# Decoder layer on one core: first sequence's loads moved ahead of the front's end, late gates held back, filter tables ranked later

## The chip, the cores and the metric

The kernel runs on one core of one Trainium2 chip. Its time is the device time of one execution in microseconds (us). Before the change three runs gave 2112.03, 2112.74 and 2116.0 us; the median is 2112.74.

An engine works through its own instructions in order. The names used are PE (TensorE, the matrix engine), DVE (VectorE), ACT (ScalarE), POOL (GpSimd) and SP (SyncE, which here only issues transfers). Everything is in 32-bit floats.

## What is computed

The input x holds 16 sequences of 512 tokens with 256 channels. Each sequence goes through three blocks, each followed by a residual add and a layer norm:

```
z    = rmsnorm(u, pre_norm_w) @ in_proj_w.T          # 768 channels
z    = causal conv of length 3 along time + bias     # per channel
x2, x1, v = split(z, 3)
h    = sum_s residues[:, s] * exp(log_poles[:, s] * t)
y    = causal_conv(x1 * v, h) + x1 * v * D_skip      # 512 taps, per channel
y    = (y * x2) @ out_proj_w.T + u
x    = layernorm(x + y + mlp(rmsnorm(y, post_norm_w)))
x    = layernorm(x + self_attention(x) + cross_attention(x, ctx))
x    = layernorm(x + low_rank_mlp(x))
```

The long convolution (y) is the only step that is done for all sequences together: channel by channel, with the times of all 16 sequences as columns.

## The kernel before

**Two programs in a row.** The *front* (L368 to L966) computes x1 * v and the gates x2 for all sequences, then the long convolution, and leaves the results in DRAM: `yconv` (one tensor for each half of 128 channels, called half 0 and half 1 here) and `gates`. The *main part* (L970 on) takes the sequences one after another through the rest: it loads x, gate and y of a sequence (L1097 to L1100), multiplies y by the gate (`times_gate`, L1103), projects (`outp`, L1117), adds x (`add_op`, L1067), and goes on to the norm, the MLP (L1143 and L1195), attention and the last MLP.

**The planner.** Each program is written as a list of operations with engines, a cost, a priority (a low number goes first), the buffers read and written, and sometimes extra dependences (`after`). `Plan.schedule` (L103) places them with these costs: each engine takes its first startable operation by priority, a buffer class such as `"x"` has a fixed number of tiles, and a tile is given back when its last user is done. What comes out is a fixed order of instructions for each engine; on the chip every engine follows its list, and waits where something isn't ready. The costs and priorities thus set the order, and nothing else.

**The front's work.** For each sequence b, `prepare` (L440) loads x, norms and transposes it into xT, a tile of class `"x"` (ten tiles `fx` of 4 KB a partition). `project` (L473) makes 128 of the 768 channels: four matmul records on PE (L479), one pass on ACT (L486), two on DVE (L494). `x1v` (L502) makes two projections for one half of the channels, multiplies them on POOL (L506), transposes on PE (L512) and copies into `xv0` or `xv1`. `gate_of` (L523) makes the two gate projections and stores them (L535).

The first seven sequences are done whole, with priorities 100 b and below. The last nine (LATE) get half 0 first; half 1 and their gates follow at 3000 + 100 b. Of these nine, sequences 7 to 10 park xT in DRAM (`normed`, L551) and read it back (L562); 11 to 15 (KEPT) hold their tile. The gates of 14 and 15 (LAST) come at the very end, behind the last matmul of the convolution (L776).

The tables: `h` is built from 16 exponentials on ACT for each half (L613) and as many multiply-adds on DVE (L623, first step L621), at priority 160, and stored in DRAM as `hpad`. The convolution works in eight blocks of 32 channels, four for each half (loop at L648). A block loads four tables (`toe`, 512 KB each, L661, on SP) into tiles of class `"x"`, or into the space of xv0 in the last block; POOL zeroes their acausal triangle (L671, "cut" below); PE makes the states of earlier chunks (`near_mm`, L686), the triangular part (L737) and the part from the states (`far_mm`, L749, "far field"). ACT and DVE copy the result out of PSUM (L301, L299), and SP, in the last three blocks ACT too, stores it (L768).

**Queues.** SP issues nearly all transfers in the order of the plan, and waits at its head where one isn't ready. The main part's first loads stand behind the front's last stores.

## Time and profile before

| | |
|---|---|
| median of three runs | 2112.74 us |
| the profiled execution's own time | 2110.95 us |
| its span, first to last instruction | 2109.2 us |
| mean granted PE clock | 0.987 |
| PE busy | 2013.7 us, 95% of the span |
| DVE, ACT, POOL busy | 62%, 48%, 36% |
| last front matmul ends, first main matmul starts | 283.03 us, 292.07 us |
| second add of the first sequence (L1067) | 298.86 us |

Times in the timeline count from the span's start. A row of a timeline has start, duration, engine, line, operation, out<-in, shapes and count; the bracket at its end is the time for which the engine idled before it, and what it waited for. In the list of waits the numbers are us in total, times, longest. In the table by windows the columns after the window are its length, the busy time of PE, PE's weight loads, DVE, ACT and POOL with counts, the granted PE clock, the DMA engines' mean busy share, and GB/s.

The page's 40 slices are 52.7 us each. PE stands at 9 tenths from the eighth slice on; slices 5, 6 and 7 (211 to 369 us) hold 8, 7 and 8, and in slice 6 the granted clock's row has an 8. This is the end of the front and the start of the main part.

### The profile page before, as it was taken

How to read it: one execution, taken by the hardware profiler on the slowest of the kernel's cores; microseconds unless marked ns; L12 is line 12 of the kernel's file. 1: busy time of each engine (PE TensorE's matmuls, PEld its weight loads, DVE VectorE, ACT ScalarE, POOL GpSimd, SP SyncE). 2: the span in 40 equal slices, each digit the busy share in tenths (PEclk: the TensorE clock that was granted, in tenths of full speed). 3: DMA queues.
4: the chain of work that ended last, by engine and by line, in shares of the span. 5: the costliest groups of instructions: out<-in, count | busy, mean ns of one | idle time of the engine just before them, and what ended most of it. 6: DMA issues, size and time to landing. Idle time of an engine off the chain costs nothing.

```text
span 2109.2 us, 35600 instructions
## 1 busy us (share of the span) xinstructions
PE 2013.7 (95%) x14324; PEld 1034.7 (49%) x14324; DVE 1317.1 (62%) x1899; ACT 1020.7 (48%) x1414; POOL 758.2 (36%) x1020
## 2 busy tenths in 40 slices
PE   8899878999999999999999999999999999999977
PEld 4455545444554545454545454544545454545433
DVE  7976522736584848484847575766656675746463
ACT  7764521565426262717172626262535354466664
POOL 6785522243424241414141424242323232334342
PEclk9999989999999999999999999999999999999999
DMA  5366861030304040313131313222221313030300
GB/s 190 112 199 210 272 191 50 1 122 17 117 11 140 14 132 22 122 32 120 34 109 45 106 48 93 61 86 68 72 81 61 93 49 95 19 105 22 102 11 21
DMA packets 114935, 182.16 MB, mean 86 GB/s; under 512 B 13393, under 2 KB 62034, under 8 KB 114642
## 3 DMA queue, kind: packets, MB, share of 16 engines
q1 hardware_dynamic: 113234, 177.26, 27.0%
q10 hardware_dynamic: 1536, 2.62, 0.4%
q8 instruction: 113, 1.85, 0.4%
q14 instruction: 52, 0.43, 0.1%
HBM read 111.09 MB, written 68.76 MB: 85 GB/s over the span
## 4 chain that ended last, share of the span: by engine, by line
PE 81%; ACT 7%; POOL 4%; DVE 3%; issue 3%; DMA 2%; SPq 0%; ACTq 0%; POOLq 0%; DVEq 0%
PE mm L1143 14%; PE scores L1387 10%; PE mm L1296 9%; PE mm L1195 8%; PE scores L1491 7%; PE av L1526 7%; PE mm L1716 4%; PE mm L1224 3%; PE av L1732 3%; PE mm L1056 3%; PE fmm L479 2%; ACT ex L1503 2%; PE mm L1118 2%; PE mm L348 2%; PE mm L1578 2%
## 5 line engine op out<-in xcount | busy, mean ns | idle before, releaser
L1503 ACT ACTIVATE ex<-scores 128x2048 f32<-128x2048 f32 x160 | 300.2, 1876 | 165.4 <-PE scores L1491 161.3
L1143 PE MATMUL mm<-xT,w_l 128*128 128x512 f32 x640 | 298.1, 607 | 0.0
L1514 POOL TENSOR_SCALAR_AFFINE_SELECT ex<-ex 128x512 f32<-128x512 f32 x256 | 158.6, 638 | 355.2 <-ACT ex L1503 330.8
L1387 PE MATMUL scores<-keys,q 32*128 32x320 f32 (+4 forms) x2560 | 224.2, 455 | 11.8 <-ACT ex L1406 10.4
L1491 PE MATMUL scores<-q,keys 32*128 32x512 f32 (+3 forms) x2048 | 185.0, 464 | 17.3 <-ACT ex L1503 14.2
L1724 ACT ACTIVATE row<-mm,b_s 128x512 f32<-128x512 f32 x128 | 81.0, 685 | 233.0 <-PE mm L1716 232.9
L1143 PEld LDWEIGHTS mm<-xT,w_l 128*128 128x128 f32 x640 | 114.9, 190 | 143.7 <-issue 130.8
L1387 PEld LDWEIGHTS scores<-keys,q 32*128 32x128 f32 x2560 | 113.0, 184 | 147.2 <-issue 48.0
L1660 POOL TENSOR_TENSOR nd<-nd,nd 128x1024 f32<-128x1024 f32 x30 | 70.8, 2361 | 307.4 <-DMA nd<-di 307.4
L479 PE MATMUL fmm<-fx,inw 128*128 128x512 f32 x384 | 176.5, 602 | 4.1 <-DVE xv L299 1.5
L1526 PE MATMUL av<-ex,va 128*32 128x512 f32 (+3 forms) x2048 | 170.8, 442 | 0.0
L1432 DVE TENSOR_TENSOR scores<-scores,mask_qk 128x1024 f32<-128x1024 f32 x144 | 126.2, 876 | 63.8 <-PE scores L1387 60.6
L308 POOL TENSOR_SCALAR small<-small 128x4 f32<-128x4 f32 (+1 forms) x66 | 13.3, 201 | 423.0 <-DVE small L1026 393.7
L494 DVE SCALAR_TENSOR_TENSOR frow<-fmm,cw,frow 128x511 f32<-128x511 f32 x192 | 140.5, 744 | 37.7 <-ACT frow L486 33.5
L1195 PE MATMUL mm<-w_l,gT 128*128 128x256 f32 x640 | 160.8, 386 | 0.0
L1155 ACT ACTIVATE row<-mm 128x512 f32<-128x512 f32 x80 | 47.8, 598 | 223.9 <-PE mm L1143 223.9
L1491 PEld LDWEIGHTS scores<-q,keys 32*128 32x128 f32 x2048 | 90.0, 185 | 117.4 <-ACT ex L1503 42.2
L299 DVE COPY row<-av 128x512 f32<-128x512 f32 x68 | 47.1, 692 | 157.9 <-PE av L1526 136.2
L1195 PEld LDWEIGHTS mm<-w_l,gT 128*128 128x128 f32 x640 | 117.8, 190 | 47.3 <-issue 33.7
L1041 ACT ACTIVATE xt<-xt,small 128x256 f32<-128x256 f32 x192 | 103.1, 595 | 76.6 <-POOL small L1034 76.6
L1302 DVE TENSOR_SCALAR q<-mm,bqc_s 128x512 f32<-128x512 f32 x62 | 46.5, 751 | 140.6 <-PE mm L1296 140.6
L1296 PE MATMUL mm<-xT,wqc_s 128*128 128x512 f32 x256 | 129.3, 617 | 0.0
(194 smaller groups left out, 3475.4 us busy)
## 6 DMA issues: line engine op xcount, KB each, us to landing
dn<-row SPq DMA_DIRECT2D x120, 256.0 KB
keys<-dk SPq DMA_DIRECT2D x64, 256.0 KB
nd<-dn SPq DMA_DIRECT2D x30, 512.0 KB
nd<-di SPq DMA_DIRECT2D x30, 512.0 KB
fx<-hpad SPq DMA_DIRECT2D x28, 512.0 KB
xt<-in_x SPq DMA_DIRECT2D x16, 512.0 KB
gate<-gates SPq DMA_DIRECT2D x16, 512.0 KB
yt<-yconv SPq DMA_DIRECT2D x32, 256.0 KB
```

Of the source, the lines that this page charges most:

```text
L479: nc.tensor.matmul(ps.t, inw[:, k, bass.ts(m, P)], xT.t[:, k, :], start=(k == 0), stop=(k == KD - 1))
L494: lambda e, lag=lag: nc.vector.scalar_tensor_tensor(t.t[:, lag:], ps.t[:, 0 : T - lag], cw[:, m, 2 - lag : 3 - lag], t.t[:, lag:], ALU.mul ...
L1041: nc.scalar.activation(x.t[:, c, :], x.t[:, c, :], AF.Identity, bias=st[:, c, 9:10], scale=st[:, c, 8:9])
L1143: nc.tensor.matmul(ps.t, w[:, k, bass.ts(f, P)], zT.t[:, k, :], start=(k == 0), stop=(k == KD - 1))
L1195: nc.tensor.matmul(ps.t[:, bass.ts(cc, D)], gT.t[:, f, bass.ts(c, P)] if f < NF else gE.t, w_l3[:, f, :] if f < NF else w_l3e[:, c, :], st ...
L1296: nc.tensor.matmul(ps.t, w[:, k, cols], xT.t[:, k, :], start=(k == 0), stop=(k == KD - 1))
L1387: nc.tensor.matmul(sc.t[:, r, at : at + hi - lo], q.t[hd, bass.ts(i, P)], kk.t[hd, lo:hi], start=True, stop=True,)
L1432: nc.vector.tensor_tensor(diag, diag, mask, ALU.add)
L1491: nc.tensor.matmul(sc.t[:, r, at : at + T - j * P], keys[g].t[hd, TC + j * P : TC + (j + 1) * P], qas[g].t[hd, j * P :], start=True, stop= ...
L1503: lambda e, sc=sc, ex=ex: nc.scalar.activation(ex.t.rearrange("p (r n) -> p r n", r=HPG), sc.t, AF.Exp, scale=scale),
L1514: lambda e, ex=ex, at=at: nc.gpsimd.affine_select(out=ex.t.rearrange("p (r n) -> p r n", r=HPG)[:, :, at : at + P], in_=ex.t.rearrange("p ...
L1526: nc.tensor.matmul(av[g].t[bass.ts(r, SLOT), j * P :], va.t[:, j, h * VS : h * VS + SLOT], ex.t[:, r * T + at : r * T + at + n], start=(j ...
```

## The change

Four things are edited, all in the front and at its border.

1. Three lasting tiles, `early`, are opened ahead of the front. During the front they serve as the xT tiles of sequences 11, 12 and 13, and class `"x"` has seven tiles instead of ten. In the main part they are the one `gate` tile, the one `yt` tile and one of the five `xt` tiles, so the memory in use is the same.
2. At the end of the front's plan, x of sequence 0, its gate and half 0 of its y are loaded into them on SP (priority 5460), each after the last reader of the xT that the tile held; the main part's own loads for these three are empty. Half 1 of y is still a load of the main part.
3. The gates of sequences 10 to 13 get the priority 4700 + 100 b, 5700 to 6000, instead of 4000 to 4300. The blocks of half 1 have about 5400 to 5700.
4. The tables' exponentials, multiply-adds and stores get the priority 500 instead of 160.

```diff
+    early_ = ctx.enter_context(tc.tile_pool(name="early", bufs=1))
+    early = tiles(early_, "early", 3, [P, NT * D])
...
-            "x": tiles(fp_, "fx", 10, [P, R8 * P]),
+            "x": tiles(fp_, "fx", 7, [P, R8 * P]),
+            **{f"e{n}": [t] for n, t in enumerate(early)},
...
-        def as_xT():
-            return View("x", lambda t: t.rearrange("p (k n) -> p k n", k=KD))
+        def as_xT(b):
+            n = b - (B - KEPT)
+            return View(f"e{n}" if 0 <= n < 3 else "x", lambda t: t.rearrange("p (k n) -> p k n", k=KD))
...
-                gate_of(b, xT, 3000 + b * 100)
+                gate_of(b, xT, (3000 if b < B - LAST - 4 else 4700) + b * 100)
...
-                    160, r=[(LP, 0)], w=[ee],
+                    500, r=[(LP, 0)], w=[ee],
...
-                plan.op("DVE", 0.32, add, 160, r=[ee, (LP, 1), (LP, 2)], w=[h])
+                plan.op("DVE", 0.32, add, 500, r=[ee, (LP, 1), (LP, 2)], w=[h])
...
+        for n, (dst, src, deps) in enumerate((
+            (early[0].rearrange("p (c d) -> p c d", c=NT), x[0].rearrange("(c p) d -> p c d", p=P), ()),
+            (early[1], gates[0], (stores[0][1], stores[1][1])),
+            (early[2].rearrange("p (k j t) -> p k j t", k=KD, j=NT)[:, 0],
+             yconv[0][:, 0].rearrange("j p t -> p j t"), Y[0]),
+        )):
+            plan.op(
+                "SP", 0.6, lambda e, dst=dst, src=src: nc.sync.dma_start(out=dst, in_=src), 5460, w=[Buf(f"e{n}")],
+                lat=4.0, after=[*deps, *(o for _, o, _ in late_T[LATE - KEPT + n][1].seen)],
+            )
...
-        "yt": tiles(kept, "yt", 1, [P, KD, T]),
-        "gate": tiles(kept, "gate", 1, [P, KD * T]),
+        "yt": [early[2].rearrange("p (k n) -> p k n", k=KD)],
+        "gate": [early[1]],
...
-        "xt": tiles(kept, "xt", 5, [P, NT, D]),
+        "xt": [early[0].rearrange("p (c d) -> p c d", c=NT), *tiles(kept, "xt", 4, [P, NT, D])],
...
-        plan.op("SP", 0.5, load_x, p0 - 500, w=[x_], lat=4.0)
-        plan.op("SP", 0.5, load_g, p0 - 500, w=[gate], lat=4.0)
-        for k in range(KD):
+        plan.op("SP", 0.5, load_x if b else lambda e: None, p0 - 500, w=[x_], lat=4.0)
+        plan.op("SP", 0.5, load_g if b else lambda e: None, p0 - 500, w=[gate], lat=4.0)
+        if not b:
+            plan.op("SP", 0.5, lambda e: None, p0 - 500, w=[(yt, 0)], lat=4.0)
+        for k in range(0 if b else 1, KD):
             plan.op("SP", 0.5, lambda e, k=k: load_y(e, k), p0 - 500, w=[(yt, k)], lat=4.0)
```

`Y[0]` are the stores of half 0's `yconv`, `stores[0]` and `stores[1]` those of the gate of sequence 0.

More of the change, by code (lines that the diff above doesn't have):

```diff
@@ L468, in prepare @@
             scale_ops(x_, sq, pr - 120, "POOL" if b else "DVE")
-            xT = transposed(x_, lambda t: t, pr - 120, as_xT())
+            xT = transposed(x_, lambda t: t, pr - 120, as_xT(b))
             marks.append(plan.ops[-1])
@@ L558, in decoder_layer @@
             if b < B - KEPT:
-                xT = as_xT()
+                xT = as_xT(b)
                 plan.op(
@@ L627, in add @@
                         nc.vector.tensor_tensor(h.t[:, P - 1 : P], h.t[:, P - 1 : P], sk[:, k : k + 1], ALU.add)
-                plan.op("DVE", 0.32, add, 160, r=[ee, (LP, 1), (LP, 2)], w=[h])
+                plan.op("DVE", 0.32, add, 500, r=[ee, (LP, 1), (LP, 2)], w=[h])
             plan.op(
-                "SP", 0.4, lambda e, k=k, h=h: nc.sync.dma_start(out=hpad[bass.ts(k, P), :], in_=h.t), 160,
+                "SP", 0.4, lambda e, k=k, h=h: nc.sync.dma_start(out=hpad[bass.ts(k, P), :], in_=h.t), 500,
                 r=[h], w=[(HPAD, k)], lat=3.0,
@@ L634, in decoder_layer @@
         plan.op(
-            "SP", 0.4, lambda e: nc.sync.dma_start(out=hpad[D : D + 1, :], in_=zero_row), 160, w=[(HPAD, KD)],
+            "SP", 0.4, lambda e: nc.sync.dma_start(out=hpad[D : D + 1, :], in_=zero_row), 500, w=[(HPAD, KD)],
             lat=3.0,
@@ L646, in decoder_layer @@
         plan.op("ACT", 0.4, lambda e: nc.scalar.activation(aT, lpT, AF.Exp, scale=float(P)), 170, r=[(LP, "T0")], w=[(NEAR, "a")])
+        Y = [[] for _ in range(KD)]
         for blk in range(NR // R8):
@@ L755, in decoder_layer, with store @@
             for c in range(HPG):
-                o = View("row", lambda t: t.rearrange("p (q u) -> p q u", u=P))
+                res = View("row", lambda t: t.rearrange("p (q u) -> p q u", u=P))
                 plan.op(
                     "ACT DVE", (act(T), dve(T)),
-                    lambda e, c=c, o=o, ys=ys: copy(
+                    lambda e, c=c, o=res, ys=ys: copy(
                         e, o.t, ys[c].t.rearrange("p (q u) -> p q u", u=P)[:, :, ::-1]
                     ),
-                    pc + 5, r=[ys[c]], w=[o],
+                    pc + 5, r=[ys[c]], w=[res],
                 )
                 for par in range(2):
-                    def store(e, at=x0 + c * R8 + par * R8 // 2, par=par, kh=kh, o=o):
+                    def store(e, at=x0 + c * R8 + par * R8 // 2, par=par, kh=kh, o=res):
                         eng = nc.sync if e == "SP" else nc.scalar
@@ L771, in store @@
                         )
-                    plan.op("ACT" if par and blk >= NR // R8 - 3 else "SP", 0.6, store, pc + 10, r=[o], lat=3.0)
+                    o = plan.op("ACT" if par and blk >= NR // R8 - 3 else "SP", 0.6, store, pc + 10, r=[res], lat=3.0)
+                    Y[kh].append(o)
+        for n, (dst, src, deps) in enumerate((
[8 more added lines that the diff above has]
+            )
         for b, xT in last_gates:
```

## The prediction

> **What bounds the kernel now.** I read the page's first part, then the list of what PE waited for in the first 310 us, then the chain of waits and PE's timeline there.

> ```profile
> PE 2013.7 (95%) x14324; PEld 1034.7 (49%) x14324; DVE 1317.1 (62%) x1899; ACT 1020.7 (48%) x1414; POOL 758.2 (36%) x1020
> ```

> PE is busy for 95% of the span, so a gain must come out of the other 95 us or out of a low clock. By the built order the main part (from L1118 on) has the same PE instructions in the same sequence in both kernels; only tile names differ. All that can change lies before 300 us. PE's waits there:

> ```profile
> PE mm L1118 <- DVE yt L1105: 9.0, 1, 9.0
> PE fmm L348 <- DVE fx L333: 8.4, 2, 7.1
> PE fmm L512 <- POOL frow L506: 6.9, 7, 3.2
> ...
> PE fmm L686 <- issue: 2.5, 1, 2.5
> ```

> The largest is one wait of 9.0 us between the last front matmul and the first main one. The 8.4 us are the start, which stays. The third is mostly one place, which PE's timeline shows together with the first:

> ```profile
> 241.62 0.66 PE L512 MATMUL fmm<-ident,frow 128*128 128x128 f32 x4 [1.07 <-POOL frow L506]
> 245.44 1.12 PE L512 MATMUL fmm<-ident,frow 128*128 128x128 f32 x4 [3.16 <-POOL frow L506]
> 247.78 2.79 PE L686 MATMUL fmm<-xv,near 128*32 128x48 f32 x128 [1.22 <-DVE xv L299]
> ...
> 274.76 1.21 PE L749 MATMUL fmm<-xv,state 16*64 16x128 f32 x64
> 275.90 7.13 PE L479 MATMUL fmm<-fx,inw 128*128 128x512 f32 x16
> 292.07 6.75 PE L1118 MATMUL mm<-outw,yt 128*128 128x256 f32 x16 [9.04 <-DVE yt L1105]
> ```

> At the switch from channel half 0 to half 1 PE idles 1.07 + 3.16 + 1.22 = 5.45 us: no other projection is left to fill it. At the end, only four projections (7.1 us) stand between the last far-field group (its end, 275.97, is called t0) and the main part. The chain of waits says what was late:

> ```profile
> 236.12 6.80 DMA fx<-hpad
> ...
> 243.08 0.87 POOL fx L671
> ...
> 244.13 1.27 POOL frow L506
> 245.44 1.13 PE fmm L512 x4
> ...
> 283.62 7.53 DMA yt<-yconv
> ```

> First: a POOL product (L506) stands behind a POOL triangle cut (L671), which waits 6.80 us for a table. Second: the first sequence's loads are issued only at 282.6, and its y takes 7.53 us with 1.5 MB asked for at once.

> **The change, part by part.** Count from the second add of the first sequence (DVE L1067), 298.86 = t0 + 22.9; its followers keep their order.

> (a) End of the front. In the built order seven projections, not four, follow the last far-field group: one of sequence 12, two of 13, then 14 and 15. Warm ones cost 8.75/5 = 1.75 us, so PE is fed to t0 + 12.2; the three moved ones take 5.3 us out of the stretch before t0. SP now issues x in the middle of the last stores, the gate after the projection of 12 (t0 + 1.8), half 0 of y after those of 13 (t0 + 5.3), and only half 1 of y as a main load. What queues there: three last yconv stores stand behind the gate load on SP, and the half-0 load behind a gate store that needs DVE. Four ACT stores took 3.12 us (277.43) and held ACT's next projection by 2.7, so I put the ACT pass of 12's at t0 + 2.4, DVE's first pair at t0 + 3.2 to 4.7, the half-0 issue at t0 + 7, and the half-1 issue, behind two more gate stores, at t0 + 8.6. The landing of 256 KB alone is read from the key round trip, a store and then the load that waits for it:

> ```profile
> 353.34 0.65 SPq L1343 DMA_DIRECT2D dk<-row  x1
> 357.52 0.81 SPq L1349 DMA_DIRECT2D keys<-dk  x2
> 359.38 0.63 SPq L1343 DMA_DIRECT2D dk<-row  x1
> ...
> 364.48 0.80 SPq L1349 DMA_DIRECT2D keys<-dk  x2
> ```

> That is 4.2 and 5.1 us; the other end is the 7.53 above. The new loads share the queue with small stores, not with 2.5 MB of x, so I take 5.1: half 0 at t0 + 12.1, half 1 at t0 + 13.7. DVE's order is 9 of the 14 passes (0.74 each), product of half 0 (0.69), two passes, product of half 1, three passes, adds. So the half-0 product ends at 12.8, two passes at 14.3, the half-1 product at 15.0. Two of eight matmul steps need half 0 alone; the other six take 2.6 us warm (0.22 a matmul, as L1195's 20 in 4.48) or 5.1 at the cold rate of 292.07 (6.75/16); I take 3.9. Second add at t0 + 18.9 to 19, DVE being free at 17.2. Gain 22.9 - 19.0 = 3.9, plus the 5.3 = **9.2 us**. With 4.2 us and a warm clock the same working ends at t0 + 17.0, a gain of 11.2; with 7.5 and cold at 22.5, a gain of 5.7.

> The cold rate comes from rows:

> ```profile
> 245.00:250.00 5.00, 3.33 (x117) 2.96 (x120) 1.60 (x2) 0.00 (x0) 3.53 (x5) 0.50 0.96 391
> 265.00:270.00 5.00, 5.00 (x82) 4.88 (x75) 0.56 (x1) 0.00 (x0) 4.69 (x9) 0.74 0.85 225
> 292.00:296.00 4.00, 3.93 (x9) 3.17 (x10) 0.69 (x1) 0.00 (x0) 0.00 (x0) 0.50 1.09 359
> ```

> The third column from the end is the granted clock: 0.50 after the 9.04 us, but also after the 3.16 us gap, and 0.74 after 2.49 us of "issue". [...]

> (b) The switch. Sequence 10's two and 11's two gate projections (7.0 us) now stand around the last two transposes, and on POOL both last products come ahead of the cuts of half 1, so the 6.80 us DMA no longer stands before them. Before, the chain from the last projection (240.56) to L686 (247.78) took 7.2 us, of which 5.45 idle; with 7.0 us more work laid in it I leave 0.5 idle: 4.9. L686 at 2.79 for 128, where the warm run at 175.49 took 1.57, gives 1.2 more. **6.1 us**, between 2.3 (the 3.16 us wait and the low clock stay) and 6.7.

> (c) Tables behind five sequences. 32 exponentials (0.396 each) and 32 DVE steps (0.41) are only moved: 12.1 us of ACT, 13.5 us of DVE, from 20 to 66 us to about 30 to 110. PE's idle places in that stretch are 0.79 (36 us) and 5.43 (55 to 72 us). DVE is 36 of 40 us busy from 40 to 80, but 16.6 of 20 after, so half of it comes back as new waits: **3 us**, between 0 and 6. The first table is needed at 133, so its lateness costs nothing up to there.

> (d) Fewer tiles for the tables' blocks. fx has 7 tiles for 10; the three early ones hold sequences 11 to 13 until their gates are done. By the built order half 0's 16 loads turn through four tiles (fx0, 1, 5, 6) and half 1's 12 through five. PE's work in half 0 is then 16 x 0.98 + 4 x 1.2 + 3.4 + 17.5 + 2.6 = 44 us, 2.75 per load, 11 us a turn; less use 1.0, cut 1.1, issue 0.5 leaves 8.4 us for a landing, above the 6.80. In half 1 the shortest turn is about 8 us: 6.4 for the landing, just under 6.80. The trace doesn't show these rings. Now POOL's cuts wait 12.2 us in all for table landings, of which PE sees 0.7 (L737 on POOL); so the cost lies between 0 and 12.2. With tight turns at 6.80 I take a third: **-4 us**. A gain is excluded, since no tile is freed sooner.

> (e) The 2.49 us of "issue" at 260.8 comes in a run of over 150 short matmuls; the new order breaks some of these runs up. I take 0 (0 to 2.5 gained).

> Edits at nothing: loads of x and gate leave the main queue, the same bytes; lasting tiles take the place of the same three.

> Sum: 9.2 + 6.1 + 3 - 4 = 14.3 us. The profiled execution took 2110.95 (span 2109.2 and 1.75 around it), 1.8 below the median 2112.74. From the median: 2098.4, **2098**. Its own range is 2089 to 2107, two thirds of the way to either end of the terms: all best gives 11.2 + 6.7 + 6 + 2.5 = 26.4 (2086), all worst 5.7 + 2.3 - 12.2 = -4.2 (2117).

> **Rivals.**
> Give-back (0.17): the rings cost 8 us instead of 4, the tables bring nothing, the switch 4: 9.2 + 4 - 8 = 5.2, so 2107.5. For it: the DMA share is already 0.96 to 1.00 from 236 to 250. Against: eight gate projections, 2 MB of stores, leave half 0.
> The loads are late anyway (0.09), so that the change doesn't do what it says: half 1 of y stands on SP behind stores and gates, the idle 9 us comes back and eats (a): 14.3 - 9.2 = 5.1, so 2107.6. For it: four stores took 3.12 us at 277.43. Against: PE is fed 5.3 us longer than before.
> Starved rings (0.09), slower: table landings so slow that PE stands at L737. Place: the six turns (four in half 0, two in half 1). It takes the whole gain when the rings lose 14.3 + 4 = 18.3 us, and makes the kernel slower by over 0.2% from 22.5: 3.8 a turn, that is a landing of 8.4 + 3.8 = 12.2 us, where the longest in the chain is 6.80. Time from 2117; with a us more a turn 2123.

> **Chances.** Forecast 0.65. What a measurement of this kernel can tell from no change is about 0.2%, 4.2 us: faster means below 2108.5. That holds the forecast and about half of the two cases near 2107.5: 0.78; within 0.13; slower 0.09. The range reaches from 2088 to 2110, over those two cases, and leaves out the starved one and the ends.

> **What would show it.** Right: the wait of L1118's successor under 4 us; seven projections before it; L686 of half 1 at about 1.6 us for 128, no L512 wait over 2 us near it; the second add near 284.5. Wrong: L737 (or its heir) waiting on POOL for more than 2 us at a time: (d) too small; the first main DVE product waiting for its DMA past t0 + 16: (a); waits of L479 on DVE between 60 and 130 us: (c).

## The result, and the profile after

| | before | after |
|---|---|---|
| median of six runs side by side | 2112.39 us | 2101.86 us |
| lowest and highest | 2111.25, 2116.0 us | 2099.65, 2106.41 us |
| the profiled execution's own time, its span | 2110.95, 2109.2 us | 2099.65, 2097.9 us |
| second add of the first sequence | 298.86 us | 286.66 us |
| from the second add to the end of the span | 1810.3 us | 1811.2 us |

The changed kernel is faster: the ratio of the times is 0.9951 with a 95% interval of [0.994, 0.9961], so 10.5 us by the medians. The profiled execution of after is the fastest of its six; a second profile of the same kernel (below) is the slowest of its five. In after the heirs of the lines named in the prediction are L485 (projection), L518 (transpose behind L512's product), L694 (near), L745 (triangle), L757 (far field), L1129 (product with the gate), L1142 (first main matmul) and L1088 (add).

PE's busy time changed little, from 2013.7 to 2010.4 us, as it should where only waits go.

What PE waited for in the first 310 us of after (us in total, times, longest):

```profile
PE mm L1142 <- DVE early L1129: 5.7, 1, 5.7
...
PE fmm L745 <- issue: 4.3, 3, 2.0
PE fmm L518 <- POOL frow L512: 3.3, 3, 1.8
...
PE fmm L745 <- POOL fx L679: 1.3, 1, 1.3
```

The 9.0 us wait ahead of the main part is 5.7, and the 6.9 us behind POOL's products are 3.3. The line "issue", in which PE waits for nothing that the profile names, has grown. PE's timeline at the two places of the prediction:

```profile
231.89 1.88 PE L485 MATMUL fmm<-early,inw 128*128 128x512 f32 x4
233.70 1.57 PE L694 MATMUL fmm<-xv,near 128*32 128x48 f32 x128
...
262.93 5.42 PE L485 MATMUL fmm<-early,inw 128*128 128x512 f32 x12
268.18 7.03 PE L485 MATMUL fmm<-fx,inw 128*128 128x512 f32 x16
280.90 5.72 PE L1142 MATMUL mm<-outw,early 128*128 128x256 f32 x16 [5.69 <-DVE early L1129]
```

The near group of half 1 follows a projection with no bracket, so with no idle time, and takes 1.57 us for 128 where it took 2.79. Behind the last far-field group (t0 is now 263.00) there are seven projections instead of four. But main's first matmul still waits 5.69 us. The chain of waits says what for, and SyncE's timeline why it was late:

```profile
268.38 7.03 DMA early<-gates
...
275.48 4.54 DMA early<-yconv
```

```profile
267.59 0.65 SPq L776 DMA_DIRECT2D yconv<-frow  x1
268.38 1.00 SPq L792 DMA_DIRECT2D early<-gates  x1
...
272.90 0.72 SPq L541 DMA_DIRECT2D gates<-frow  x1
275.48 0.38 SPq L792 DMA_DIRECT2D early<-yconv  x1
...
277.44 0.37 SPq L1107 DMA_DIRECT2D early<-yconv  x1
```

The gate's load (512 KB) is issued 5.4 us behind t0, right behind stores that SyncE was still issuing until 268.24, and lands 7.03 us later. Half 0 of y is issued just then, 12.5 us behind t0. Two things stood before it: stores, the last of which was issued by 273.62 (t0 + 10.6), and then the gate's load itself, for which SyncE waited at half 0's issue (us in total, times, longest):

```profile
SPq L792 <- DMA early<-gates: 1.8, 1, 1.8
```

Half 0 does not read the gate. But in this trace SyncE's 634 transfers step eight semaphores, the gate's load and half 0's step the same one (number 106), and the 1.8 us are a wait for that one. Half 1 comes 2 us later, behind the last two gate stores.

Cut at the milestones, the two profiled executions give this ledger. A projection more or fewer done before a milestone is counted at 1.72 us.

| stretch | before | after | projections moved out | gain |
|---|---|---|---|---|
| start to the first near group of half 0 | 175.49 | 170.52 | 1 | 3.25 |
| on to the near group of half 1 | 72.29 | 63.18 | 3 | 3.95 |
| on to t0 | 28.19 | 29.30 | -1 | 0.6 |
| t0 to the second add | 22.89 | 23.66 | -3 | 4.4 |

The sum is 12.2 us, and 0.9 us of it is lost in the main part. By the prediction's own signs: seven projections stand before the main part, the near group of half 1 takes 1.57 us, and no wait for a product is over 2 us at the switch; but the wait ahead of the main part is not under 4 us, and the second add stands at 286.66 instead of 284.5.

### The profile page after: what moved, and what is told of

Same layout as the page of the kernel before. It is cut to its first block, busy times and chain, and to the rows that moved or that the text cites. A ratio compares the mean times of both kernels' runs of the same rounds, so it can differ in the third digit from the quotient of the medians.

```text
span 2097.9 us, 35560 instructions
## 1 busy us (share of the span) xinstructions
PE 2010.4 (96%) x14324; PEld 1031.2 (49%) x14324; DVE 1324.8 (63%) x1906; ACT 1015.8 (48%) x1407; POOL 756.1 (36%) x1020
## 3 DMA queue, kind: packets, MB, share of 16 engines
q8 instruction: 113, 1.85, 0.4%
## 4 chain that ended last, share of the span: by engine, by line
PE 86%; ACT 6%; POOL 2%; DVE 2%; issue 2%; DMA 2%; SPq 0%; ACTq 0%; POOLq 0%; DVEq 0%
PE mm L1167 14%; PE scores L1411 10%; PE mm L1320 9%; PE mm L1219 8%; PE scores L1515 8%; PE av L1550 7%; PE fmm L485 6%; PE mm L1740 4%; PE mm L1248 3%; PE av L1756 3%; PE mm L1077 3%; ACT ex L1527 2%; PE mm L1142 2%; PE mm L348 2%; PE mm L1602 2%
## 5 line engine op out<-in xcount | busy, mean ns | idle before, releaser
L1515 PE MATMUL scores<-q,keys 32*128 32x512 f32 (+3 forms) x2048 | 185.6, 466 | 17.2 <-ACT ex L1527 14.2
L308 POOL TENSOR_SCALAR small<-small 128x4 f32<-128x4 f32 (+1 forms) x66 | 13.1, 199 | 419.3 <-DVE small L1047 390.4
L299 DVE COPY row<-av 128x512 f32<-128x512 f32 x68 | 47.0, 691 | 158.2 <-PE av L1550 140.2
L485 PE MATMUL fmm<-fx,inw 128*128 128x512 f32 x312 | 142.7, 601 | 0.0
L1430 ACT COPY ex<-scores 128x2048 f32<-128x2048 f32 x48 | 89.5, 1865 | 55.3 <-PE scores L1411 48.3
```

The costliest lines, as they stand in the source:

```text
L485: nc.tensor.matmul(ps.t, inw[:, k, bass.ts(m, P)], xT.t[:, k, :], start=(k == 0), stop=(k == KD - 1))
L1430: "ACT", act(HPG * T), lambda e, sc=sc, both=both: nc.scalar.copy(both.t, sc.t), ps_ - 6,
L1515: nc.tensor.matmul(sc.t[:, r, at : at + T - j * P], keys[g].t[hd, TC + j * P : TC + (j + 1) * P], qas[g].t[hd, j * P :], start=True, stop= ...
```

## The experiments

All times are medians; ratios are to the kernel before, run on the same chip. That kernel's medians were 2112.37, 2112.59 and 2112.76 us in the three groups of runs. The first four kernels do one part alone or leave one out.

**One part alone: the tables.** The kernel before with edit 4 only.

```diff
-                    160, r=[(LP, 0)], w=[ee],
+                    500, r=[(LP, 0)], w=[ee],
```

(The multiply-adds and stores likewise.)

> The kernel before with one part of the change: the tables' exponentials, multiply-adds and stores at priority 500 instead of 160. My theory: the parts add up, and the tables are worth what the two traces show up to the first L686 of half 0 (175.49 against 170.52 us, less one projection of 1.7 us): 3.2 us, so 2109 against 2112.4 before, with L686 of half 1 still slow (about 2.8 us for 128) and the 9 us wait at the end unchanged. Rival: the tables earn nothing alone, since PE's waits at 55 to 72 us come back at 80 to 130: 2112. Second rival: the new order of the whole front that any changed priority brings is what pays: 2105 or less.

2111.91 us, ratio 0.9995 [0.9987, 1.0004]. The first near group starts at 172.37 against 175.49, with one projection (1.72 us) fewer done, so 1.4 us are gained there; but the wait ahead of the main part grew from 9.0 to 10.1 us and the second add stands at 298.23. Alone, edit 4 earns nothing that can be measured; the time is that of the first rival, and the theory's 2109 is out.

**One part alone: the held gates.** The kernel before with edit 3 only.

```diff
-                gate_of(b, xT, 3000 + b * 100)
+                gate_of(b, xT, (3000 if b < B - LAST - 4 else 4700) + b * 100)
```

> The kernel before with one part of the change: the gates of sequences 10 to 13 at priority 4700 + 100 b; ten fx tiles and all main loads as before. My theory: the idle 5.5 us at the switch of the halves and most of the low clock behind it go (about 4.5), and the three projections that now stand behind t0 cover part of the wait for the loads, which are issued later too: 3 more; together 2105. Rival: held gates only move the idle time to the end, where the loads start as much later as the projections last: 2108 or more, with a wait at L1118 of 9 us as before.

2108.7 us, ratio 0.9978 [0.9968, 0.9989]. PE's timeline of this kernel:

```profile
233.91 1.57 PE L686 MATMUL fmm<-xv,near 128*32 128x48 f32 x128
...
266.30 12.28 PE L479 MATMUL fmm<-fx,inw 128*128 128x512 f32 x28
287.43 5.40 PE L1118 MATMUL mm<-outw,yt 128*128 128x256 f32 x16 [8.85 <-DVE yt L1105]
```

The idle time at the switch of halves is gone, and the near group is at 1.57: held gates alone do that. At the end seven projections (12.28 us) now follow t0, and the wait is still 8.85: main's loads were issued at 275.91, later against t0 than before, since they stand behind the stores of the held gates. So at the end held gates alone only move the idle place along, as the rival said; in all they earn 3.7 us.

**All but the tables.** The changed kernel with edit 4 undone.

```diff
-                    500, r=[(LP, 0)], w=[ee],
+                    160, r=[(LP, 0)], w=[ee],
```

> The changed kernel with the tables back at priority 160; the rest as changed. My theory, parts that add up: 3.2 us slower than the changed kernel, 2105. Rival, tables worth nothing: 2102. If the tables were the whole gain of the front it would be 2109.

2107.43 us, ratio 0.9978 [0.997, 0.9987]: 5.6 us above the changed kernel, against 0.5 that the same edit earned alone. The first near group starts 4.7 us later (175.18), one projection more being done, so 2.9 us are lost there against that profile (1.7 against a second profile of the changed kernel, below). In half 1, 2.9 us of "issue" appear, at a place where such a wait lasted 0 to 3.17 us in other versions with the tables late (below). The stretch from t0 to the second add is about as long as in the changed kernel (23.8 us). None of the three times expected was met, 2107.43 lying between two of them. So the parts do not add up, and a part's worth depends on which others are there.

**All but the early loads.** The changed kernel without edit 2; the lasting tiles stay, and x, gate and both halves of y are main's own loads.

```diff
-        for n, (dst, src, deps) in enumerate((
...
-                "SP", 0.6, lambda e, dst=dst, src=src: nc.sync.dma_start(out=dst, in_=src), 5460, w=[Buf(f"e{n}")],
...
-        for k in range(0 if b else 1, KD):
+        for k in range(KD):
```

> The changed kernel without the three early loads: the lasting tiles, seven fx tiles, held gates and tables stay, PE's order is the same, and x, gate and both halves of y of the first sequence are loaded by the main part. My theory: the end gains from the early loads even though the gate's load landed late; four loads at 276 to 278 us land after about 8 us, so the first L1129 product stands near 285 instead of 280 and the kernel takes 2106 to 2107. Rival: the end's gain comes from the three held projections alone, and the early gate load is what makes half 0 late: 2102 or below, the same as the changed kernel.

2106.17 us, ratio 0.9972 [0.9962, 0.9983], above the changed kernel by 4.3, as the theory expected, but not for its reason: from t0 (267.97) to the second add it took 23.4 us, no more than the 23.66 of the changed kernel. The first product with the gate starts at 282.81, t0 + 14.8, where the changed kernel has t0 + 17.1. Its queue shows why: with the lasting tiles main's own load of x moved up to 243.52, the gate to t0 + 7.3, and half 0 of y to t0 + 8.7, ahead of where the early loads put it.

**The gate's load earlier.** The changed kernel with the tiles dealt out anew; x is loaded by main, behind half 1 of y.

```diff
-            (early[0].rearrange("p (c d) -> p c d", c=NT), x[0].rearrange("(c p) d -> p c d", p=P), ()),
-            (early[1], gates[0], (stores[0][1], stores[1][1])),
-            (early[2].rearrange("p (k j t) -> p k j t", k=KD, j=NT)[:, 0],
+            (early[0], gates[0], (stores[0][1], stores[1][1])),
+            (early[1].rearrange("p (k j t) -> p k j t", k=KD, j=NT)[:, 0],
```

> The changed kernel with the three lasting tiles dealt out anew: the gate of the first sequence goes into the tile of sequence 11, which is free at the switch to main, half 0 of y into the tile of sequence 12, and x is loaded by main behind half 1 of y. TensorE's order is that of the changed kernel. Theory (the 7.03 us of the late gate load, for which half 0 of y waited, made the first term short): half 0 of y is issued 5.5 to 7 us after the last far-field group instead of 12.5, the first product for main comes some 4 us earlier, the second add stands 20 to 21.5 us after that group instead of 23.66, and the time is 2 to 3 us under the changed kernel's, near 2099. Rival (half 1 of y, behind the last stores of gates, sets the end by itself): second add at 23 to 24 us, time within 1 us of the changed kernel's, or above it where x stands behind half 1.

2099.72 us, ratio 0.9942 [0.9929, 0.9955]. SyncE's timeline, with t0 at 267.90:

```profile
258.42 0.58 SPq L791 DMA_DIRECT2D early<-gates  x1
...
273.08 0.63 SPq L791 DMA_DIRECT2D early<-yconv  x1
...
280.39 0.37 SPq L1106 DMA_DIRECT2D early<-yconv  x1
```

Half 0 is issued at t0 + 5.2, a little earlier than expected, its product starts at t0 + 9.8, and the second add stands at t0 + 21.8 (20 to 21.5 expected), 1.9 us sooner than in the first profile of the changed kernel and 3.4 sooner than in the second. Half 1 is now what comes last (t0 + 12.5). The test changes two things at once: the gate's load is no longer ahead of half 0, and half 0, in the tile of sequence 12, stands further up the queue, ahead of three stores of y and two of gates. By the times it is 1.3 us under the changed kernel's pooled median (below), which is within the spread.

**Another load ahead of half 0.** The changed kernel with the gates of sequence 12 ahead of those of 11, so that x's load and not the gate's is the late one.

```diff
-                gate_of(b, xT, (3000 if b < B - LAST - 4 else 4700) + b * 100)
+                gate_of(b, xT, (3000 if b < B - LAST - 4 else 4300 if b == 12 else 4700) + b * 100)
```

> The changed kernel with one priority changed: the gates of sequence 12 come at the switch of halves and those of sequence 11 late, so that the gate load goes early and the load of x, also 512 KB, becomes the late one. If half 0 of y is held by whichever 512 KB load stands ahead of it on the queue, it is issued again 11 to 13 us after the last far-field group, and the time stays within 1 us of the changed kernel's. If it is the gate's own data that the first product waits for, the first product comes 2 to 4 us earlier and the time is 2 us lower, near 2100.

2104.87 us, ratio 0.9968 [0.9957, 0.9979], slower than the changed kernel by 3 to 4; neither expectation held whole. Half 0 was issued 6.06 us behind x's load (272.25, then 278.31); but x's load itself went out sooner, at t0 + 2.4, the stores ahead of half 0 were through at 277.51, only 0.8 us before half 0 went out, and the first product ended its wait 13.1 us behind t0 (269.82) instead of 17.1. The gain was lost at once: on DVE the last passes of the gates stood behind that product, and PE waited for one of them:

```profile
PE mm L1142 <- DVE frow L500: 4.3, 1, 4.3
```

From t0 to the second add it takes 24.0 us, so the 3 to 4 us were lost before t0. The stretch from the near group of half 1 to t0 takes 36.2 us here, and 29.3 in the first profile of the changed kernel; waits named issue make 6.6 us of it here and 3.1 there. What these waits are comes below.

**Late stores on another queue.** The changed kernel with ScalarE's queue taking second-half stores from one block earlier.

```diff
-                    o = plan.op("ACT" if par and blk >= NR // R8 - 3 else "SP", 0.6, store, pc + 10, r=[res], lat=3.0)
+                    o = plan.op("ACT" if par and blk >= NR // R8 - 4 else "SP", 0.6, store, pc + 10, r=[res], lat=3.0)
```

> The changed kernel with ScalarE's queue also taking the second-half stores of the fourth block from the end, which in the changed kernel stood on SyncE's queue behind loads of tables that waited for TensorE (7.6 us in two waits). If those late stores hold back the last copies and so the loads that follow, the copies that waited 3.09 and 1.73 us for stores wait under 1 us, the second add comes 1 to 3 us earlier and the time is 1 to 3 us lower, 2099 to 2101. Rival (the last copies are early enough): within 1 us, 2101 to 2103.

2100.56 us, ratio 0.9948 [0.9934, 0.9962]: the gate's load was issued at t0 + 4.2, half 0 at t0 + 8.9, and the second add stood at t0 + 22.3 (t0 is 262.78). As expected, the last copies of DVE no longer wait for stores. The stretch is 1.4 us shorter than in the first profile of the changed kernel; the times can't tell the two apart.

**The changed kernel again.**

> The changed kernel itself once more, for the spread of its profiled executions: 2102 by the median. If the unexplained idle time of TensorE (named issue in the waits, 0.80, 0.57 and 1.55 us in the second half of the near-field before) belongs to the order of the program, it comes back at the same places with the same lengths; if it varies from one execution to the next, it is found at other places or with other lengths, up to the 3.17 us of the version without the early loads.

2101.01 us, ratio 0.9942 [0.9928, 0.9957]. With the first six, eleven runs have a median of 2101.01 us. In this profile t0 is 267.12 and the second add stands 25.2 us behind it. The order of PE is the same as in the first profile, where t0 is 263.00. The idle times named issue sit at the same matmuls with other lengths. First profile, then second:

```profile
239.37 2.23 PE L745 MATMUL fmm<-fx,xv 128*64 128x128 f32 x37 [1.55 <-issue]
...
259.59 0.37 PE L757 MATMUL fmm<-xv,state 16*64 16x128 f32 x2 [0.57 <-issue]
```

```profile
241.19 3.86 PE L745 MATMUL fmm<-fx,xv 128*64 128x128 f32 x37 [2.17 <-issue]
...
263.71 0.38 PE L757 MATMUL fmm<-xv,state 16*64 16x128 f32 x2 [1.12 <-issue]
```

In both executions the first stands behind 42 block products, and the second before the last 2 of a far-field group of 64. The stall before the 47th of a near group was 1.21 and 0.66 us; that before the 49th was not there in the first profile and 0.45 us in the second.

**The program shifted.** What are these stalls? The changed kernel with 32 transposes more at the head of PE's program, and nothing else moved.

```diff
+                for _ in range(8):
+                    ps = Buf("mm")
...
+                        for c in range(NT):
+                            nc.tensor.transpose(ps.t[:, bass.ts(c, P)], ident, ident)
...
+                    plan.op("PE", 0.0, turn, -2000, w=[ps])
```

> The changed kernel with 32 more transposes (of the identity, into accumulators that nobody reads) at the head of TensorE's program; all that follows is in the same order. In all runs of this order so far the idle time named issue sits at the same matmuls, with lengths from 0.3 to 3.2 us: before the 47th of the 64 matmuls of one near group, the 43rd of the block products behind the near group of half 1, the 49th of a near group of 64, and the 63rd of a far-field group of 64. Counted along TensorE's program these stand 528, 378 and 126 matmuls apart. Theory (TensorE waits for its own instructions, which come in blocks of a fixed size of some 126 to 128 matmuls with their weight loads): each of these stalls moves 32 matmuls ahead, to the 15th, the 11th, the 17th and the 31st. Rival (each stall is a wait for data that the profile doesn't name, or belongs to the place in the program): the stalls stay at the 47th, 43rd, 49th and 63rd. Time: 2101 by either, up to 3.9 us more if the 32 transposes at 0.12 us lie bare.

2104.04 us, ratio 0.9956 [0.994, 0.9971]. Behind the near group of half 1, PE now stops after 11 block products instead of 42:

```profile
233.54 0.87 PE L754 MATMUL fmm<-fx,xv 128*64 128x128 f32 x11
238.04 5.63 PE L754 MATMUL fmm<-fx,xv 128*64 128x128 f32 x69 [3.63 <-issue]
```

That stall moved 31 matmuls ahead. The other three are gone, and so is one that the expectation leaves out (1.97 and 1.99 us, behind 28 block products of half 0); 32 matmuls ahead of their places nothing is seen. Three others appeared: 0.21 us before the second matmul of a group of block products, 0.20 us before the 63rd of the last far-field group, and 0.51 us before 16 block products at 262.49. So one of the four moves that the theory named came. Its distances also hold an error: from the 47th to the 43rd it is 504 matmuls, four times 126, not 528.

A count over all traces decides. Take PE's own instructions in their order: matmuls, weight loads and waits on semaphores. The 13 profiles of this case have 65 idle times of PE over 0.12 us named issue. Of these 54 come with 1473 or 1474, 1985, 2242, 3265 or 3266, 3522, 3777 or 3778, 4034, 4289 or 4546 instructions before it, whatever the version. Each of these counts leaves 193 or 194 when divided by 256. So the stalls belong to a count of 256 instructions, about 126 matmuls with their weight loads, and not to data. The queues' part of the after page says what is fetched (packets, MB, share):

```profile
q8 instruction: 113, 1.85, 0.4%
```

1.85 MB in 113 packets are 16.4 KB each. The traces hold the time of each packet of this queue:

| profile | PE stops | packet starts, ends | PE goes on |
|---|---|---|---|
| after | 237.81 | 236.95, 237.95 | 239.37 |
| the changed kernel again | 239.02 | 238.81, 239.72 | 241.19 |
| the program shifted | 234.41 | 235.77, 236.68 | 238.04 |
| without the early loads, again (below) | 254.30 | 255.31, 256.28 | 257.48 |

All 54 stalls end 0.9 to 1.6 us behind the end of such a packet. So, by these times and counts, what PE waits for is its own program, and a stall is long where the packet comes late; in these runs of short matmuls it lasted up to 3.63 us. The other 11 do not belong here: 0.80 to 0.86 us before the block products behind a near group, in ten profiles, which stays at its place in the shifted kernel too, and the 0.51 us above. What they wait for is open.

**Without the early loads, again.**

> The version of the changed kernel without the early loads, once more. Its median was 2106.17, against 2101.0 for eleven runs of the changed kernel, though counted from the last far-field group its second add came no later (23.4 us against 23.66 and 25.16). If the early loads earn those 5 us: 2105 to 2107 again, with the last far-field group some 3 us later than in the changed kernel. If the difference was the spread of executions: 2100 to 2103.

2103.9 us, ratio 0.9958 [0.9946, 0.9971]. t0 is 267.33, and the second add stands 23.4 us behind it, as in the first run of this version. The time lies between the two expectations. By the medians the early loads earn some 3 to 5 us, and none of it behind t0. The profiles show it ahead of t0: from the near group of half 1 to t0 this version takes 33.7 and 33.0 us, and the changed kernel, the tiles dealt out anew, the late stores and both together (below) take 28.5 to 32.2. Both profiles of this version have one stall in common:

```profile
257.48 0.38 PE L694 MATMUL fmm<-xv,near 128*32 128x48 f32 x16 [3.17 <-issue]
```

It is 3.17 us in both, and 0, 0.45, 0.29, 1.78, 1.40 and 0.85 us in the six unshifted profiles of versions with tables ranked late and early loads. Main's load of x goes out at 243.52 in the first profile of this version, between the tables' loads, where the early load waits until 255.81. That x's 512 KB crowd out the instructions there is argued, not shown: with the tables early (and x at 261.21) the stall was 2.90 as well, and the packet itself took 0.95 us, no longer than at short stalls; it started late. The stall also costs behind its end: the next 48 block products take 4.51 us in both profiles, at a granted clock of 0.65 and 0.57, and 2.84 us at 1.00 behind the stall of 0.85.

**Both shorter ends together.** The tiles dealt out anew and the stores on ScalarE's queue.

> The changed kernel with both edits that shortened the stretch behind the last far-field group: gate in the first tile, half 0 of y in the second and x loaded by main (21.76 us from that group to the second add, where the changed kernel had 23.66 and 25.16), and the second-half stores of the fourth block from the end on ScalarE's queue (22.29 us). If they add up: 20 to 21 us, and a time near 2098. Rival (both shorten the same wait, the late half 1 of y): 21.5 to 22.5 us and 2099.5 to 2101.

2099.45 us, ratio 0.9931 [0.9919, 0.9944], the fastest version measured. From t0 (264.08) to the second add it takes 20.3 us, so the two edits add up in this stretch, as expected; the time is 1.5 us above the 2098 expected, at the rival's lower end. DVE's timeline there:

```profile
279.67 0.68 DVE L1131 TENSOR_TENSOR early<-early,early 128x512 f32<-128x512 f32 x1
280.27 3.62 DVE L500 SCALAR_TENSOR_TENSOR frow<-fmm,cw,frow 128x510 f32<-128x510 f32 x5
283.81 1.28 DVE L1087 TENSOR_TENSOR y<-mm,early 128x512 f32<-128x512 f32 x2
```

No row has a bracket: DVE no longer waits for y, but works through the last gates' passes without a gap up to the adds, and PE waits 2.3 us for one of them. DVE is what sets the end now. The version's interval overlaps that of the changed kernel's rerun (0.9928 to 0.9957), so it isn't shown to beat that kernel.

## Why the prediction was right, and where it was wrong

The direction was right, and the time lies within the range. The forecast of 14.3 us was 3.8 above the 10.5 measured (2.9 above the 11.4 of the eleven runs). The forecast's own range is not what its words say: two thirds of the way from 2098.4 to the ends 2086 and 2117 is 2090 to 2111, not 2089 to 2107. Term by term:

**(a), the end of the front: 9.2 forecast, 4.4 and 2.9 measured.** This is the term that was mis-sized. The 5.3 us of moved projections came, but the 3.9 us of the shorter stretch did not. Set against seven projections, the stretch of the kernel before would be 22.89 + 5.16 = 28.1 us. Held gates alone give 26.5, the lasting tiles (with late tables) on top 23.4 and 23.4, and the early loads on top of these 23.7 and 25.2: no gain. The step that failed is "the gate after the projection of 12 (t0 + 1.8)" with "the half-0 issue at t0 + 7". The gate's load was issued at t0 + 5.4, behind late stores of y: the last copies of DVE waited 3.09, 1.36 and 1.73 us for earlier stores to free their buffers, and in the built order the last stores wait for these copies. The stores ahead of half 0 ended at t0 + 10.6, 3.6 us later than the forecast had it, and the wait for the gate's load held it for another 1.9 us, to t0 + 12.5 (10.7 and 12.0 in the second profile). The prediction had counted the stores behind the gate's load but not the lateness of those ahead of it, and it had not looked at the landing that an issue itself waits for. Its sign for this failure was given: the first main product waiting for its DMA past t0 + 16. It ran at t0 + 17.1. Where half 0 was issued at t0 + 5.2 (the tiles dealt out anew), the stretch fell to 21.8, and with the stores moved too to 20.3, which is near the 19.0 that (a) had worked out.

The landing itself was sized well: 5.1 us assumed for 256 KB, 4.54 measured. So were the last six matmul steps: 3.9 us assumed, 3.88 from the end of the half-1 product to the second add; in the second profile it was 5.6, over the 5.1 that the prediction gave for a cold clock.

For the matmuls behind the wait the prediction took a middle between the warm and the cold rate. In the version with the gate in the first tile, PE had only two gaps of 1.51 and 1.41 us ahead of the last 12 of main's first matmuls. The table by windows (columns as ahead of the prediction), first for that version before, around and behind the two gaps, then for the 16 behind the 5.69 us gap of after:

```profile
274.00:279.00 5.00, 5.00 (x13) 2.22 (x12) 3.84 (x7) 3.19 (x5) 0.00 (x0) 1.00 1.00 315
279.00:284.00 5.00, 2.21 (x7) 0.87 (x5) 4.11 (x8) 0.78 (x1) 0.00 (x0) 0.94 0.67 220
284.00:289.60 5.60, 5.47 (x12) 3.87 (x12) 4.24 (x7) 1.29 (x3) 0.00 (x0) 0.50 0.99 308
```

```profile
281.00:287.00 6.00, 5.62 (x16) 3.92 (x16) 4.88 (x8) 1.52 (x4) 0.00 (x0) 0.69 0.91 267
```

The granted clock, third from the end, is 1.00 before and 0.50 behind the two short gaps. Here gaps of 1.4 to 1.5 us in a thinly filled stretch (PE busy for 2.21 of 5.00 us) did not leave the matmuls behind them warm.

**(b), the switch of halves: 6.1 forecast.** The idle time went from 5.45 us to 0 and the near group from 2.79 to 1.57, which is 6.7, the upper end of the bounds. The held gates alone show the same lines.

**(c), the tables: 3 forecast.** The pair of profiles gives 3.25 up to the first near group, so the size looked right. Over all profiles it is less: with early tables that group starts at 175.18 to 176.70 us (three profiles), with late ones at 170.52 to 172.65 (nine, without the shifted program), 3.9 us apart in the mean, or 2.2 without the projection of 1.72. And alone the edit earned 0.5 us, and taken out of the changed kernel it cost 5.6. The step that failed is the sum itself, which gave the tables one price whatever else is changed.

**(d), fewer tiles: -4 forecast.** PE's waits for POOL's cuts and products at L745 rose from 0.7 to 1.5 us, under 1 us lost. The rings did not starve; the third rival is out.

**(e), "issue": 0 forecast.** "The new order breaks some of these runs up" was wrong, as the stalls go by the count of instructions. Stalls sum to 4.7 us in the profile of before, and 6.1 and 7.2 in those of after (the 0.8 us of open cause included): 1.4 to 2.5 us lost, outside the bounds of 0 to 2.5 gained. That they change from one execution to the next also blurs every comparison of two single profiles: t0 differed by 4.1 us between two executions of the same program.

So of the gain that was forecast and did not come, the end of the front accounts for 4.8 us in the first pair of profiles; (b) and (d) came out better than forecast and (e) worse. That the time lies near is in part luck: the 3.1 us by which (d) was put too high made up for most of what (a) lacked. With the pair's own figures the terms come to 4.4 + 6.7 + 3.25 - 0.9 - 1.4 = 12.05 us of the ledger's 12.2. The give-back rival's 2107.5 us was not reached. The second rival was half right: the loads were late, more for the stores that it named than for the wait on the gate's load, and the idle place kept 5.69 of its 9.04 us.

## What to carry to other kernels

A load moved ahead is worth what its own issue waits for: follow the stores ahead of it on its queue back to what they wait for, see in the queue's own waits whether the landing of another transfer holds it (1.8 us here), and put the large transfer where it can't hold the small one that is needed first. Tiles that outlive a stage may bring main's loads forward by themselves (26.5 to 23.4 us here, with late tables as well), so ask what the added load still adds. Where single profiles of one program differ by 4 us, a part is judged by medians of several runs, and a part's worth alone (0.5 us) is not its worth beside the others (5.6 us).

## What the runs showed of the hardware

TensorE's granted clock fell from 1.00 to 0.50 after two gaps of 1.51 and 1.41 us with two matmuls between them (the version with the gate in the first tile).

In the changed kernel SyncE held the issue of a 256 KB load for 1.8 us until a 512 KB load ahead of it on the same queue had landed (1.2 us in the second profile); in the first trace both loads step one semaphore. The later one went out 7.1 and 6.45 us behind the gate's, the stores between them taking the rest. With x's 512 KB in the gate's place it went out 6.06 us behind, 0.8 us after the last store between them.
